# Third attention layer: scores from exact high and low parts, and one list that orders all work between attention blocks

## Chip, cores and metric

The kernel runs on one core of one Trainium2 chip. The metric is device time in microseconds (us) of one execution, here the median of three runs. A profile is of one execution of its own, and its times count from the start of that execution's span.

The engines by the names of the profile: PE is TensorE's matmul, PEld its weight load, DVE is VectorE, ACT is ScalarE, POOL is GpSimd, and SP is the engine that issues most DMAs. SPq and POOLq are the queues of DMA issues.

## What is computed

The reference is a stack of three attention layers and an MLP, on 16 sequences of 256 tokens with 256 features, with 16 heads of 16 features. Cut to what matters:

```
layer 0:  q from rmsnorm(x), k and v from rmsnorm(ctx)
          x = rmsnorm(x + attention(q, k, v) @ Wo)
layer 1:  h = layernorm(x); q, k, v from h, with bias; rope on q and k
          x = x + attention(q, k, v, causal) @ sa_wo + sa_bo
layer 2:  h = layernorm(x); q from h, k and v from ctx, with bias; rope on q and k
          x = x + attention(q, k, v) @ ca_wo + ca_bo
MLP:      x + gelu(layernorm(x) @ fc1 + b1) @ fc2 + b2
```

All inputs and outputs are 32-bit floats. "Third layer" below means layer 2.

## The kernel before

**Tiles.** A sequence b has three attentions, one for each layer, so there are N_ATT = 48 attentions. The digits of ORDER give the layer of each in turn; attention i works on the next sequence of its layer. Sequences at different layers are interleaved, so that one attention's chain of small steps runs beside another one's matmuls. After the 48 attentions eight MLP groups of two sequences follow, from about 700 us on.

**One attention.** `q` and `k` project with `by_feature` (L354), `v` and `project` with `by_token` (L366): 32 records of TensorE each. In layers 1 and 2 `rotated` applies the rope: two biased copies from PSUM on ACT (L475), then on DVE a shuffle (L479) and two products with tables (L483); the sum follows at L514 for q and L591 for k.

The scores of an attention are worked out in blocks: four in layers 0 and 2, three in the causal layer 1. A block ends in two tiles S of two PSUM banks each, and the pool has just two of these. Then two exponentials on ACT (L659) write tiles pt; in layer 1 two `affine_select` on POOL (L666) cut the upper triangle. `values` (L687) multiplies pt with v into tile A; a copy takes it to SBUF (L702).

What follows is a chain through DMAs: `heads_in` (L708) sorts the heads into oT, `sums_in` (L719) takes the softmax sums, `invert` inverts them on DVE (L735) and spreads them through DRAM (L737, L743), and `divide` multiplies (L749). `project` adds the result to x (L755 in layer 0, L758 in the others). For layers 1 and 2 the next attention of the sequence begins with statistics (L266, L267, root on POOL L248 and L249), `norm` (L273) and a transposition, either on TensorE (L288, L298) or as 32x32 pieces on DVE and DMAs (L308, L313, L319). `keep` adds the output bias on POOL (L342).

**Two forms of the scores.** Features of a pair of heads are interleaved over the partitions: even partitions belong to one head, odd ones to the other, 32 partitions to a pair. In the plain form (L637, layers 1 and 2, and the first two attentions) q is copied twice, each copy with the other head's rows set to zero (L515, L518; L522 puts the second copy on ACT), and a true 32-bit matmul of 64 keys and 512 columns gives both heads.

In the fast form (L648; layer 0 from attention 2 on, which `FAST = (0,)` and `fast(i)` choose) k is split exactly into a high part, rounded to the one-pass format float32r, and the rest (`k_high` L553 on ACT, `k_low` L557 on DVE), q likewise (`q_high` L528 on ACT, `q_low` L535 and L538 on DVE). DMAs put the two parts of q (`q_out` L544) and of k (`k_out` L565) in the rows that the masks zeroed. A one-pass matmul of 128 keys and 256 columns then sums, in its 32 rows, both parts of one head's k with one part of its q; two of them (h = 0 and 1) give all four products of that head (i):

```python
for i in range(2):
    at = m * (2 * u + i)
    for h in range(2):
        for r, ps in rows:
            nc.tensor.matmul(
                ps[:, at : at + m],
                lhsT=self.kd[r, i, t, kc * P : (kc + 1) * P].bitcast(F32R),
                rhs=self.qd[r, i, h, t, q0:S].bitcast(F32R),
                start=(h == 0), stop=(h == 1), skip_group_check=True,
            )
```

**What sets the order.** The body stands in `tc.manual_schedule()`: each engine runs its instructions in the order in which the program names them, and semaphores add the waits between engines. The order of the attention stage comes from the loop over i and n (block n of attention i): after `scores(n)` come `values(n - 1)`, and then whole steps of neighbours, by conditions such as `finishing`, `late`, `fresh`, `shifted`, `hasty`. `turned_ahead` chooses which attentions are transposed in pieces. `load_next` issues loads on POOL (L1136) when their turn comes. A step such as `q` is issued as a whole, with its PE, ACT and DVE instructions one after the other.

If a count of softmax sums at the end were too small, a general branch (`shifted_layers`) would run. None of its instructions is in the trace.

Of the kernel before, what the change touches and what calls it, by code (L numbers as in the profile page):

```python
# [30 lines left out]
FAST = (0,)  # L31
# [22 lines left out]

def turned_ahead():


    slots = {}

    def place(j, tried):  # L60
        for m in range(j - 3, max(attended(j)[1] + 2, j - 8), -1):
            if ORDER[m] != 1 and m not in tried:
                tried.add(m)
                if m not in slots or place(slots[m], tried):
                    slots[m] = j
                    return True
        return False

    for j in range(N_ATT):
        if ORDER[j] > 0:  # L70
            place(j, set())
    return slots
# [3 lines left out]
def xattn_kernel(  # L76
# [120 lines left out]
    def fold_bias(items):  # L197

        ps = dense_ps()
        for k in range(KC):  # L200
            for j, (t, at, vcol) in enumerate(items):
                nc.tensor.matmul(
                    ps[32 * j : 32 * j + 32, :D],
                    lhsT=vec[:, vcol + k : vcol + k + 1].to_broadcast([P, 32]),
                    rhs=t[:, k, at : at + D],
                    start=(k == 0), stop=(k == KC - 1), skip_group_check=True,
                )
        sb = work.tile([P, 2 * D], F32, tag="a", name="fold")
        nc.scalar.copy(sb[:, :D], ps[:, :D])
        hop = dram.tile([4, D], F32, tag="fold", name="fold_hop")  # L210
        nc.sync.dma_start(out=hop, in_=sb[0:P:32, :D])
        return hop
# [49 lines left out]
    def ln_stats(src):  # L262
        st = small.tile([P, NC, 6], F32, tag="bst", name="bst")
        mv = small.tile([P, NC, 2], F32, tag="bmv", name="bmv")
        for c in range(NC):
            nc.vector.bn_stats(st[:, c, :], src[:, c, :])  # L266
            nc.vector.bn_aggr(mv[:, c, :], st[:, c, :])  # L267
        return mv, inv_sqrt(mv[:, :, 1], EPS_LN, "ln")
# [25 lines left out]
    def turned(src):  # L294

        ps = turn_ps(src)
        t = turn_tile()
        nc.scalar.copy(  # L298
# [3 lines left out]
        return t  # L302

    def pieces_out(xn):

        t = work.tile([P, 4, KC, NC, 32], F32, tag="a", name="turn")
        for k in range(KC):
# [3 lines left out]
            )  # L311
        hop = dram.tile([P, 4, KC * NC * 32], F32, tag="turn", name="turn_hop")
# [65 lines left out]
    class Att:  # L378
        def __init__(self, i):
            self.i = i  # L380
            self.layer = ORDER[i]
            self.b, self.below = attended(i)
            self.causal = self.layer == 1
            self.w = (w0_sb, sa_sb, ca_sb)[self.layer]
# [12 lines left out]
            self.fast = fast(i)  # L397

        def stats_x(self):
            self.pad = pads[self.b % 2]  # L400
            self.rx = self.pad[0][:, :NC]
            inv_sqrt(mean_squares(self.x, "x"), EPS_RMS, "x", self.rx)

        def stats_y(self):
            self.ry = inv_sqrt(mean_squares(ys.pop(self.b), "y"), EPS_RMS, "y")
# [3 lines left out]
        def stats(self):  # L409
            if self.layer == 0:  # L410
                self.stats_x()
                self.stats_y()
            else:
                self.mv, self.r = ln_stats(self.x)

        def spread(self):
# [3 lines left out]
            for c in range(NC):  # L420
                for j in range(0, P, 32):
# [4 lines left out]
                    )  # L426
            nc.scalar.copy(self.rq, ps[:, :S])

        def send(self):

            if self.layer == 0 and self.i > 1:
                nc.vector.transpose(self.pad[1], self.pad[0])
                self.rq_hop = dram.tile([S], F32, tag="rq", name="rq_hop")
                for c in range(NC):
                    nc.sync.dma_start(
                        out=self.rq_hop[c * P : (c + 1) * P].rearrange("(g j) -> g j", j=32),
                        in_=self.pad[1][c:P:32],
                    )

        def receive(self):  # L440
            if self.layer == 0 and self.i > 1:
                self.rq = work.tile([P, S], F32, tag="rq", name="rq", bufs=1)
                nc.sync.dma_start(out=self.rq, in_=self.rq_hop.partition_broadcast(P))

        def norm(self):
            if self.layer > 0:
                self.xn = ln_apply(self.x, self.mv, self.r, work)

        def keep(self):

            if self.layer > 0:
                add_bias(self.x, R_SAO if self.layer == 1 else R_CAO)

        def turn(self):
            if self.layer == 0:
                self.hT = xTs.pop(self.b)
            else:
                self.hT = turned(self.xn)
            self.kvT = self.hT if self.layer == 1 else yTs[self.b]

        def pieces_out(self):
            self.norm()
            self.hop = pieces_out(self.xn)

        def pieces_in(self):
            self.hT = turn_tile()
            pieces_in(self.hT, self.hop)
            self.kvT = self.hT if self.layer == 1 else yTs[self.b]

        def rotated(self, ps, n):  # L470
# [3 lines left out]
            for t in range(KC):  # L474
                nc.scalar.activation(  # L475
                    a[:, t], ps[:, t], AF.Identity, bias=bias[:, t : t + 1]
                )
            u = work.tile([P, KC, S], F32, tag="u", name="u", bufs=1)
# [3 lines left out]
            for t, table in ((a, cos_t), (u, sin_t)):  # L482
                nc.vector.tensor_tensor(  # L483
                    t, t, table.unsqueeze(1).to_broadcast([P, KC, S]), ALU.mult
                )
            return a, u
# [10 lines left out]
        def q(self, both=True):  # L497
            ps = by_feature(self.hT, self.w, 0)
            if self.fast:
                self.qd = self.query_tile()  # L500
                self.qa = work.tile([P, KC, S], F32, tag="a", name="qa")
                rq = self.rq.unsqueeze(1).to_broadcast([P, KC, S])
                nc.vector.tensor_tensor(self.qa, ps, rq, ALU.mult)
                return
            self.masked_tile()
            if self.layer == 0:
                rq = self.rq.unsqueeze(1).to_broadcast([P, KC, S])
                for i in range(2):
# [4 lines left out]
            a, u = self.rotated(ps, 0)  # L513
            nc.vector.tensor_tensor(a, a, u, ALU.add)  # L514
            nc.vector.tensor_scalar(self.qm[:, :, 0, :], a, parity[0], None, ALU.mult)  # L515
            self.rotated_q = a
            if both:
                nc.vector.tensor_scalar(self.qm[:, :, 1, :], a, parity[1], None, ALU.mult)  # L518

        def second_mask(self):  # L520
            if self.layer > 0 and not self.fast:
                nc.scalar.activation(  # L522
                    self.qm[:, :, 1, :], self.rotated_q, AF.Copy, scale=parity[1]
                )

        def q_high(self):

            nc.scalar.copy(  # L528
# [4 lines left out]
        def q_low(self):  # L533
# [3 lines left out]
            )  # L537
            nc.vector.tensor_copy(self.qd[:, 1, 1].bitcast(F32R), self.qd[:, 0, 1])  # L538
# [7 lines left out]
        def k_mm(self):  # L546
            src = yTs[self.b] if self.layer == 0 else self.kvT
            self.ps_k = by_feature(src, self.w, D)

        def k_high(self):  # L550

            self.hl = work.tile([P, 2, KC, S], F32, tag="hl", name="hl", bufs=1)
# [17 lines left out]
        def first_qk(self):  # L570
# [4 lines left out]
            ps = by_feature(self.hT, self.w, 0)  # L575
            self.spread()
            for t in range(KC):
                nc.scalar.copy(self.kT[:, t], by_feature(self.kvT, self.w, D, [t])[:, t])
            self.stats_y()
# [6 lines left out]
        def k(self):  # L586
            ps = by_feature(self.kvT, self.w, D)
            self.kT = self.key_tile()[:, 0]
            if self.layer > 0:
                a, u = self.rotated(ps, 1)  # L590
                nc.vector.tensor_tensor(self.kT, a, u, ALU.add)  # L591
            else:
                nc.scalar.copy(self.kT, ps)

        def v(self):
            ps = by_token(self.kvT, self.w, 2 * D)
            va = self.va
            if self.layer == 0:
# [3 lines left out]
                )  # L602
                for c in range(NC):
# [5 lines left out]
            else:  # L609
                row = R_SAV if self.layer == 1 else R_CAV  # L610
                nc.gpsimd.memset(va[:, :, :, 1], 1.0)
                nc.vector.tensor_tensor(
# [6 lines left out]
        def scores(self, n):  # L619
# [35 lines left out]
            for ps in pss:  # L655
                pt = work.tile([P, 2, 512], F32, tag="pt", name="pt", bufs=PT_LIVE)
# [3 lines left out]
            for u, unit in enumerate(units):  # L660
                cols = slice(2 * m * u, 2 * m * (u + 1))
                self.pts[unit] = [pt[:, :, cols] for pt in pts]
                if self.causal:
                    for pt in self.pts[unit]:
                        diag = pt.rearrange("p j (i s) -> p j i s", i=2)[:, :, :, 0:P]
                        nc.gpsimd.affine_select(  # L666
                            out=diag, in_=diag, compare_op=ALU.is_ge, fill=0.0, base=0,
                            pattern=[[0, 2], [0, 2], [1, P]], channel_multiplier=-1,
                        )

        def values(self, n):


            for unit in self.parts[n]:
                self.value(*unit)

        def value(self, t, kc):
# [15 lines left out]
            if final and t == 0:  # L693
# [3 lines left out]
                self.take(t, nc.scalar.copy)  # L697
# [6 lines left out]
        def heads_in(self):  # L704

            for t in range(KC):
                for i in range(2):
# [16 lines left out]
        def end(self, copy=nc.vector.tensor_copy):  # L724

            self.take_last(copy)
            self.sums_in()
            self.heads_in()

        def invert(self, beside=lambda: None):  # L730
# [4 lines left out]
            nc.vector.reciprocal(sums[:, 1], sums[:, 0])  # L735
# [1097 lines left out]
```

## Time and profile before

| what | value |
|---|---|
| median of 3 runs (lowest to highest) | 907.46 us (907.29 to 907.56) |
| the profiled execution, its own time | 907.57 us |
| its span | 905.9 us |
| mean granted clock of TensorE | 0.999 |
| TensorE busy, 0 to 20 us | 16.94 us |
| TensorE busy, 40 to 120 us | 76.97 us |
| TensorE busy, 200 to 220 us | 17.93 us |
| DVE busy, all | 689.5 us |
| ACT busy, all | 541.4 us |
| exponentials, layers 1 and 2 (224) | 217.1 us, 1022 ns each |
| exponentials, layer 0 (128) | 135.7 us, 1114 ns each |
| DMA share, mean of 40 to 120 us | 0.51 |

A group's row in the profile reads: line, engine, operation, output <- inputs, shapes, count | busy us, mean ns of one | idle time of the engine just before, and what ended it. A timeline row reads: start us, duration us, engine, line, operation, shapes, count, and in brackets the idle time before it. Consecutive matmuls overlap, so that one group's duration is longer than the step to the next group's start.

### The profile page before, as it was taken

To read this page: it belongs to the slowest core of one execution; us is meant where nothing else is said; L and a number is where in the kernel's file an instruction comes from. 1 tells how busy PE (TensorE), PEld (TensorE's weight loads), DVE (VectorE), ACT (ScalarE), POOL (GpSimd) and SP (SyncE) were. 2 spreads that over 40 slices of the span, in tenths; PEclk is the share of its full clock that TensorE was granted. 3 is DMA by queue.
4 is the path that set the end of the run, shared out by engine and by line. 5 is a ranking of instruction groups with operands and counts; after the bars stand their busy time and mean duration, and the time that the engine had idled before them with its cause. 6 is when DMAs were issued, how large, how long until landed. Compare 5 with 4: busy or idle time off the path is not lost.

```text
span 905.9 us, 32810 instructions
## 1 busy us (share of the span) xinstructions
PE 889.2 (98%) x13762; PEld 538.4 (59%) x13762; DVE 689.5 (76%) x1529; ACT 541.4 (60%) x758; POOL 339.4 (37%) x558
## 2 busy tenths in 40 slices
PE   8999999999999999999999999999999999999997
PEld 3455555445454545455455554444445799999997
DVE  4369878986778887878967889898796687777653
ACT  3776765766676766766666676666665633334440
POOL 4144765425452465244454435556133131111000
PEclk9999999999999999999999999999999999999999
DMA  8454554434243233332354322111211011112201
GB/s 268 151 180 155 169 164 154 132 107 134 79 122 103 97 114 127 95 114 63 109 165 144 119 81 67 63 55 59 62 40 38 26 65 62 54 35 68 71 25 50
DMA packets 94286, 90.26 MB, mean 100 GB/s; under 512 B 25578, under 2 KB 80754, under 8 KB 94130
## 3 DMA queue, kind: packets, MB, share of 16 engines
q1 hardware_dynamic: 89042, 73.11, 25.1%
q0 software_dynamic: 4400, 14.42, 5.4%
q8 instruction: 110, 1.80, 0.8%
q10 hardware_dynamic: 688, 0.54, 0.2%
q14 instruction: 46, 0.38, 0.1%
HBM read 46.33 MB, written 13.65 MB: 66 GB/s over the span
## 4 chain that ended last, share of the span: by engine, by line
PE 84%; DVE 7%; DMA 4%; SPq 2%; issue 1%; ACT 1%; POOL 0%; ACTq 0%; DVEq 0%
PE A L687 16%; PE d L354 16%; PE d L366 14%; PE S L637 13%; PE upX L908 6%; PE A L1006 6%; PE downZ L1006 3%; PE upZ L908 3%; PE S L648 3%; PE d L1006 2%; PE d L908 2%; DMA sums<-av 1%; DVE a L483 1%; DVE u L483 1%; DVE u L479 1%
## 5 line engine op out<-in xcount | busy, mean ns | idle before, releaser
L659 ACT ACTIVATE pt<-S 128x1024 f32<-128x1024 f32 x224 | 217.1, 1022 | 114.8 <-PE S L637 114.8
L687 PE MATMUL A<-pt,va 128*32 128x256 f32 (+1 forms) x3072 | 189.7, 367 | 0.0
L687 PEld LDWEIGHTS A<-pt,va 128*32 128x32 f32 x3072 | 80.6, 109 | 125.1 <-issue 55.2
L659 ACT ACTIVATE pt<-S,sy 128x1024 f32<-128x1024 f32 x128 | 135.7, 1114 | 26.9 <-PE S L648 18.0
L637 PE MATMUL S<-qm,kT 32*64 32x512 f32 (+1 forms) x2176 | 134.5, 559 | 4.0 <-DVE kT L591 3.3
L666 POOL TENSOR_SCALAR_AFFINE_SELECT pt<-pt 128x512 f32<-128x512 f32 x128 | 87.3, 697 | 123.8 <-ACT pt L659 122.8
L475 ACT ACTIVATE a<-d,qk_bias 128x256 f32<-128x256 f32 x128 | 53.7, 470 | 45.4 <-PE d L354 32.9
L342 POOL TENSOR_TENSOR cur<-cur,bias 128x512 f32<-128x512 f32 x48 | 67.4, 1410 | 32.9 <-DVE xn L273 32.8
L248 POOL TENSOR_SCALAR r_ln<-bmv 128x2 f32<-128x2 f32 x48 | 13.5, 281 | 158.0 <-DVE bmv L267 156.8
L637 PEld LDWEIGHTS S<-qm,kT 32*64 32x64 f32 x2176 | 34.4, 130 | 53.1 <-issue 31.9
L354 PE MATMUL d<-hT,sa 128*32 128x256 f32 x1024 | 61.1, 379 | 0.0
L930 ACT COPY g<-upX 128x512 f32<-128x512 f32 x28 | 15.0, 589 | 72.4 <-issue 67.5
L483 DVE TENSOR_TENSOR a<-a,turn 128x512 f32<-128x512 f32 x64 | 52.5, 820 | 2.2
L483 DVE TENSOR_TENSOR u<-u,turn 128x512 f32<-128x512 f32 x64 | 53.9, 842 | 0.0
L702 DVE COPY av<-A 128x512 f32<-128x512 f32 x47 | 31.8, 677 | 22.5 <-PE A L687 22.2
L479 DVE STREAM_SHUFFLE u<-a 128x512 f32<-128x512 f32 x64 | 47.8, 746 | 0.0
L946 ACT ACTIVATE g<-g,fb 128x256 f32<-128x256 f32 x96 | 41.0, 499 | 11.1 <-DVE g L935 11.1
L354 PEld LDWEIGHTS d<-hT,sa 128*32 128x32 f32 x1024 | 33.3, 110 | 22.0
L648 PEld LDWEIGHTS S<-qm,kT 32*128 32x128 f32 x896 | 30.9, 183 | 25.8 <-ACT pt L659 18.6
L648 PE MATMUL S<-qm,kT 32*128 32x256 f32 x896 | 43.2, 303 | 2.3 <-ACT pt L659 1.7
L749 DVE TENSOR_TENSOR oT<-oT,inv 128x512 f32<-128x512 f32 x48 | 36.6, 762 | 7.4 <-DMA oT<-av 5.2
L273 DVE TENSOR_SCALAR xn<-cur,bmv,r_ln 128x256 f32<-128x256 f32 x96 | 40.9, 475 | 0.3 <-POOL r_ln L249 0.3
(167 smaller groups left out, 1655.7 us busy)
## 6 DMA issues: line engine op xcount, KB each, us to landing
inv<-inv_hop SPq DMA_DIRECT2D x96, 128.0 KB
oT<-av SPq DMA_DIRECT2D x192, 64.0 KB
turn_hop<-turn SPq DMA_DIRECT2D x33, 256.0 KB
hT<-turn_hop SPq DMA_DIRECT2D x132, 64.0 KB
kT<-hl SPq DMA_DIRECT2D x28, 256.0 KB
qm<-qm SPq DMA_DIRECT2D x28, 256.0 KB
out<-res SPq DMA_DIRECT2D x15, 256.0 KB
yT<-in_yt POOLq DMA_DIRECT2D x11, 256.0 KB, 3.5
```

The source lines that it names most:

```text
L342: nc.gpsimd.tensor_tensor(t, t, bias_sb[:, row : row + D].unsqueeze(1).to_broadcast([P, NC, D]), ALU.add)
L354: nc.tensor.matmul(o, lhsT=w[:, k, at + t * P + j : at + t * P + j + 32], rhs=tokens, start=(k == 0), stop=(k == KC - 1), skip_group_check ...
L366: nc.tensor.matmul(ps[j : j + 32, c * D : (c + 1) * D], lhsT=some_tokens(src, k, c, j), rhs=w[:, k, at : at + D], start=(k == 0), stop=(k ...
L479: nc.vector.stream_shuffle(u.rearrange("p t s -> p (t s)"), a.rearrange("p t s -> p (t s)"), SWAP)
L483: nc.vector.tensor_tensor(t, t, table.unsqueeze(1).to_broadcast([P, KC, S]), ALU.mult)
L637: nc.tensor.matmul(ps[64 * half : 64 * half + 64, 2 * m * u : 2 * m * (u + 1)] .rearrange("p (i s) -> p i s", i=2), lhsT=self.kT[r, t, at] ...
L648: nc.tensor.matmul(ps[:, at : at + m], lhsT=self.kd[r, i, t, kc * P : (kc + 1) * P].bitcast(F32R), rhs=self.qd[r, i, h, t, q0:S].bitcast(F ...
L659: nc.scalar.activation(pt[:, :, :w], ps[:, :, :w], AF.Exp, scale=scale)
L666: nc.gpsimd.affine_select(out=diag, in_=diag, compare_op=ALU.is_ge, fill=0.0, base=0, pattern=[[0, 2], [0, 2], [1, P]], channel_multiplier=-1,
L687: nc.tensor.matmul(self.av[32 * r : 32 * r + 32, i, q0:S], lhsT=self.va[:, kc, 8 * t + 2 * r + i, :], rhs=pts[r // 2][:, r % 2, i * m : (i ...
L908: nc.tensor.matmul(o if len(b.shape) == 2 else by_groups(o), lhsT=a[:, c * P : (c + 1) * P], rhs=b, start=(first and c % 2 == 0), stop=Tru ...
L1006: nc.tensor.matmul(ps[:, c, :], lhsT=a[f // 2][:, f % 2, c * P : (c + 1) * P], rhs=b[:, f, :], start=(first and c == 0 and f == 0), stop=True,
```

## The change

`FAST` becomes `(0, 2)`, so the third layer takes the fast form too. Its rotated q and k are split as layer 0's are: `q` ends with the sum in tile a, which `q_high` and `q_low` read; `k` writes its sum in the second half of tile hl, `k_high` copies it rounded to the first half, and `k_low` subtracts in place. The two masks of q go in this layer. In layer 1 the second mask is always made on ACT. The tile hl, which had a second use as a buffer for combined MLP weights, loses that one; a part of w0 takes its place, and the general branch loads w0 again.

The methods become generators that yield wherever the engine changes. A string PLAN names all segments, 2,640 words, and each occurrence of a word runs the next segment of that step: `k.11` is named six times, for PE, ACT and four times DVE. The loop with its conditions goes. Transposition in pieces is chosen by the words `pieces` and `turn`, loads by `load_piece`, `load_early` and `load_later`. Start-up (to the first word) and the MLP stage keep their order.

```diff
-FAST = (0,)
+FAST = (0, 2)
...
+PLAN = """
...
+scores.43.0 heads_in.42 q.44 stats.46 values.42.2 scores.43.0 q.44 stats.46 scores.43.0 turn.45
+take_last.42 q.44 turn.45 heads_in.42 scores.43.1 q.44 k_high.44 values.43.0 scores.43.1
+sums_in.42 k_low.44 k.45 q.44 scores.43.1 norm.46 k_out.44 q_high.44 divide.41 scores.43.2 keep.46
+pieces.46 values.43.1 scores.43.2 q_low.44 pieces.46 v.44 v.44 scores.43.2 q_low.44 invert.42 k.45
+q_out.44 divide.42 scores.43.3 v.44 values.43.1 q.45 invert.42 k.45 scores.43.3 k.45 pieces_in.46
+scores.43.3 k.45 values.43.2 q.45 k.45 values.43.3 k_high.45 q.45
...
+        def q(self):
+            ps = by_feature(self.source(False), self.w, 0)
+            yield
...
+            a = self.biased(ps, 0)
+            yield
+            u = self.swapped(a)
+            yield
+            self.times(a, cos_t)
+            yield
+            self.times(u, sin_t)
+            yield
             nc.vector.tensor_tensor(a, a, u, ALU.add)
+            if self.fast:
+                self.qa = a
+                return
+            yield
+            self.masked_tile()
             nc.vector.tensor_scalar(self.qm[:, :, 0, :], a, parity[0], None, ALU.mult)
+            yield
+            nc.scalar.activation(self.qm[:, :, 1, :], a, AF.Copy, scale=parity[1])
...
+        def k(self):
...
+            if self.fast:
+                self.hl = self.high_low()
+                self.ps_k = self.hl[:, 1]
+                nc.vector.tensor_tensor(self.ps_k, a, u, ALU.add)
+                return
...
             pts = []
             for ps in pss:
+                yield
                 pt = work.tile([P, 2, 512], F32, tag="pt", name="pt", bufs=PT_LIVE)
...
-                + [work.tile([P, 2, KC, S], F32, tag="hl", name="down_t", bufs=1)[:, 0]]
+                + [w0_sb[:, 0, : 2 * D].rearrange("p (k s) -> p k s", s=S)]
...
+    def step(word):
+        if word not in steps:
+            steps[word] = begin(word) or iter(())
+        next(steps[word], None)
...
-        for i in range(N_ATT):
-            a, last = att(i), att(i - 1)
...
+        for word in PLAN.split():
+            step(word)
```

## The prediction

> **What bounds the kernel now.** I read the page first: the busy line, then the chain that ended last.
>
> ```profile
> span 905.9 us, 32810 instructions
> ...
> PE 889.2 (98%) x13762; PEld 538.4 (59%) x13762; DVE 689.5 (76%) x1529; ACT 541.4 (60%) x758; POOL 339.4 (37%) x558
> ...
> PE 84%; DVE 7%; DMA 4%; SPq 2%; issue 1%; ACT 1%; POOL 0%; ACTq 0%; DVEq 0%
> ```
>
> TensorE is busy all but 16.7 us, of which 3.1 lie in the first 20 us, and 84% of the chain is its own work. So time is worth what TensorE gets rid of, less any new wait of TensorE. The profiled execution took 907.57 us, 0.1 above the median of 907.46; its span is 905.9, so 1.7 lie around it. I count from 907.57.
>
> Next the groups of instructions, with shapes kept apart, for the two forms of the scores.
>
> ```profile
> L637 PE MATMUL S<-qm,kT 32*64 32x512 f32 x1664 | 116.6, 612 | 4.0 <-DVE kT L591 3.3 <-ACT hT L298 0.7
> L648 PE MATMUL S<-qm,kT 32*128 32x256 f32 x896 | 43.2, 303 | 2.3 <-ACT pt L659 1.7 <-DMA qm<-qm 0.5
> ```
>
> A block outside the causal layer has 16 records in either form, so 1664 records hold 104 block-sized lots (two slow first-layer attentions, the third layer, half of the causal layer) and 896 hold 56 blocks. A mean of one record hides overlap; the step is read from starts in the timeline. First a fast block of layer 0, then a block of layer 2.
>
> ```profile
> 306.66 0.75 PE L648 MATMUL S<-qm,kT 32*128 32x256 f32 x16
> ...
> 307.33 1.07 PE L687 MATMUL A<-pt,va 128*32 128x256 f32 x16
> ...
> 308.22 1.91 PE L366 MATMUL d<-sa,hT 128*32 128x256 f32 x32
> ...
> 310.06 0.75 PE L648 MATMUL S<-qm,kT 32*128 32x256 f32 x16
> ```
>
> ```profile
> 657.70 1.11 PE L637 MATMUL S<-qm,kT 32*64 32x512 f32 x16
> ...
> 658.75 1.07 PE L687 MATMUL A<-pt,va 128*32 128x256 f32 x16
> ...
> 659.64 1.91 PE L354 MATMUL d<-yT,ca 128*32 128x256 f32 x32
> ...
> 661.48 1.11 PE L637 MATMUL S<-qm,kT 32*64 32x512 f32 x16
> ```
>
> Start to start, scores, values and one projection take 0.67 + 0.89 + 1.84 = 3.40 us in the fast form and 1.05 + 0.89 + 1.84 = 3.78 in the other; the usual step of the second kind is 3.77. Nothing else in the block differs, so the form is worth 0.37 us.
>
> **The change, part by part.**
>
> *Scores.* 16 third-layer attentions x 4 blocks x 0.37 = 23.7 us less on TensorE. The instructions are those of L648 in number and shape, so this price is measured and not derived.
>
> The Trainium skill ("FP8 and Floating Point Precision", TensorE Precision Notes) says that a true FP32 product makes four passes. Two one-pass products would then halve the scores, 1.05 to an estimated 0.52, and the 64 blocks would give about 34 us and an end near 874; the rows say 0.67, and I go by them.
>
> *New work on ScalarE.* Each third-layer attention gains q_high (L528, 1.05) and k_high (L553, 0.59): 26.1 us. All 16 second masks of the causal layer now go to ScalarE (L522, 0.72: 11.6), and five masks there go (3.6). ACT ends at 541 + 34 = 575 us. In one block of 3.40 the two exponentials take 1.94 (2 x 0.97 in the timeline), which leaves 1.46, or 5.84 per attention. The rest is two bias pairs (0.84 each), one copy of av (0.60), q_high and k_high: 3.92. It fits, and so I cost it at nothing; but q_high with a second such piece does not fit in one gap.
>
> *New work on VectorE.* q_low (L535 0.69, L538 0.44) and k_low (L557, 0.68) add 1.81 per attention, 28.9 in all. The first mask (L515, 16 of 0.61) and all 27 second masks on VectorE (L518, 0.56) go: 24.9. Net +4. What hides it is TensorE's longer work, but not everywhere:
>
> ```profile
> 540.00:640.00 100.00, 98.34 (x1760) 47.09 (x1760) 91.25 (x165) 64.84 (x88) 55.00 (x69) 1.00 0.20 62
> ```
>
> Columns after the stretch and its length are TensorE, weight loads, VectorE, ScalarE, GpSimd. This stretch has 16 third-layer blocks: TensorE's 100 shrinks by 5.9 to 94.1, while VectorE goes to some 92 (four attentions, each +0.64 or a little more, less up to three masks of the causal layer). So VectorE is 98% of the new stretch. In the last run of third-layer attentions, 653.9 to 684.7 (two attentions), it is 27.5 of 30.8 before, and would be 27.5 + 1.7 = 29.2 against 30.8 - 3.0 = 27.8: 1.4 too much. For eight such attentions that bounds the loss at 5.6, if nothing is moved, and at 0, if the list moves rotations and statistics a block or two. I take 2.
>
> *New transfers.* 64 more issues on SP's queue (q_out L544, k_out L565, 0.58 to 0.62 each): 38 us on a queue that stands waiting for over 400 us in the table of waits. Where q_out waits for q_low, what stands behind it are the head copies, sums and inverses of the attention before, which divide and then project need. In the list divide comes 6.9 us of TensorE work before its project in the median, so nothing is charged. What can be late is q_out itself. The one transfer that TensorE waited for is this:
>
> ```profile
> 351.03 1.16 SPq L544 DMA_DIRECT2D qm<-qm  x2
> ...
> 355.83 0.51 PE L648 MATMUL S<-qm,kT 32*128 32x256 f32 x8 [0.49 <-DMA qm<-qm]
> ```
>
> The second half came 4.8 us after the issue began. In nine others scores started 3.8 to 4.0 after q_out and did not wait. I added up TensorE's steps between q_out.i and scores.i.0 in the list: 27 of 30 attentions have 3.8 or more (rounded), 14 have over 4.8, the shortest (attention 47) has 2.9. If all transfers took 3.8, the loss is under 2 us; if all took 4.8, it is 12.4. I take 0, since none of the other 13 transfers made TensorE wait. The one buffer of hl must be read by k_out before the next k is written to it: the same sum gives 4.3 us at least, and 2.4 is what a kT transfer takes in the chain, so nothing there.
>
> *The order.* The list names the same segments with the same durations; the only new PE instructions are the scores. Its first word is at 16.3 us, so start-up is untouched, and the MLP keeps its order. Every engine runs its words in the listed order, loads on the POOL queue and all of SP's included, so each moved step can gain or lose. TensorE's 13.6 idle us after start-up are what a better order can gain (3.0 of it between 40 and 120, 2.1 between 200 and 220, where hT came late). I summed row durations by attention over the list: VectorE never has over 3.5 us more than TensorE in a run of up to 16 blocks, ScalarE never over 2.1. That excludes an engine overrunning, not a late step. I take 2 of the 13.6 as won, which cancels VectorE's 2.
>
> *Cover by GpSimd.* An operation on VectorE with both inputs in SBUF can be stretched when GpSimd adds the bias:
>
> ```profile
> 666.33 0.69 DVE L483 TENSOR_TENSOR a<-a,turn 128x512 f32<-128x512 f32 x1
> 666.35 1.82 POOL L342 TENSOR_TENSOR cur<-cur,bias 128x512 f32<-128x512 f32 x1
> ...
> 666.94 1.78 DVE L483 TENSOR_TENSOR u<-u,turn 128x512 f32<-128x512 f32 x1
> ```
>
> 0.69 became 1.78: 1.1 us per meeting. The Trainium skill ("SBUF — State Buffer", SBUF: two separate sides) makes it an exclusive lock between a VectorE instruction with two SBUF inputs and a GpSimd one that reads SBUF. That speaks against this change: q_low and now k_low subtract SBUF from SBUF, and if each of the 32 met an add it would cost VectorE about 35 us by the measured 1.1. The 14 q_low of before took 0.68 to 0.69 each and met none.
>
> **Sum.** 907.57 - 23.7 + 2 - 2 = 883.9; I say 884.0.
>
> **Rivals.**
>
> *The list also clears the old waits.* For it: 13.6 us idle, at places with no lack of other work. Against: with 0.37 less per block every wait has less cover. Half of it gives 883.9 - 6.8 = 877. Chance 0.20.
>
> *Late query halves.* Place: the first scores of each fast attention. For: 16 margins below 4.8. Against: the 13 transfers that held nothing up. All at 4.8: 883.9 + 12.4 = 896. Chance 0.20.
>
> *Slower: ScalarE held up by q_high.* It waits for VectorE's rotation, and behind it in ScalarE's queue stand the exponentials; one block takes both score tiles, so the next scores wait too. ScalarE has 1.46 - 1.05 = 0.41 to spare in that block. VectorE late by two bias meetings (2.2) costs 1.8 in each of 16 attentions: 883.9 + 28.6 = 912.5. It decides from 23.7/16 = 1.5 of lost time per attention, a lateness of 1.9. For: VectorE at 98%, and the two buffers of a, where 7 of 99 reuses in the list come within 1.9 us of the last reader. Against: the list puts the third layer's q some 13 to 16 us of TensorE work ahead of its scores, and a path of about 10 us (0.84 + 3.3 + 1.05 + 1.1 + 3.8) leaves room. Chance 0.12.
>
> *No effect.* The list gives back just what the form saves, or the blocks keep 3.77 because scores wait for exponentials (0.87 to their start, 1.94 for them, about 0.4 to the next scores: 3.2, under 3.40). Time 907. Chance 0.03.
>
> **Numbers.** Forecast 884.0 with 0.45. The range 873 to 902: down to most of the idle recovered (0.8 x 13.6 = 10.9), up to the late halves and VectorE's whole 5.6 together (883.9 + 12.4 + 5.6); it leaves out the slower case, no effect and a little of the tails. A measurement here tells about 0.2%, 1.8 us, from no change. Faster 0.45 + 0.20 + 0.20 = 0.85; same 0.03; slower 0.12.
>
> **What would show it.** L648 should have 1920 records and L637 1152; third-layer blocks should step 3.40. A TensorE idle time near 17 us confirms the cancelling, near 10 the first rival. Late halves show as waits of the first L648 of an attention for qm; a held ScalarE as gaps of TensorE before L648 with ACT as releaser and L528 waiting for L514's line. VectorE should be over 95% busy in the stretch that ends the third layer; if TensorE is idle there by more than 5 us, my 2 us were too few. Fast blocks that step over 3.6 would break the main term.

## The result and the profile after

The changed kernel takes 905.9 us (median of 20 runs, 901.97 to 907.44); the kernel before took 909.5 beside it (20 runs, 906.73 to 912.26). The ratio is 0.9958, 95% interval 0.9947 to 0.9969: 3.8 us faster, where 23.5 were forecast. The time lies outside the range of 873 to 902. The profiled execution took 906.3 us, 1.3 less than that of before; the accounting below is of these two executions.

The page of the changed kernel, the lines that answer to those of before:

```profile
span 904.5 us, 32853 instructions
...
PE 881.5 (97%) x13762; PEld 565.6 (63%) x13762; DVE 699.5 (77%) x1534; ACT 570.8 (63%) x801; POOL 352.3 (39%) x558
...
PE 76%; DVE 9%; DMA 5%; ACT 3%; issue 3%; SPq 3%; POOL 1%; ACTq 0%; DVEq 0%; POOLq 0%
```

TensorE is busy 7.7 us less, not 23.7, and idle 23.0 instead of 16.7. Its own share of the chain fell from 84% to 76%: more steps now end in a wait for another engine. The groups of the scores, shapes kept apart:

```profile
L962 PE MATMUL S<-qm,kT 32*128 32x256 f32 x1920 | 96.4, 304 | 6.1 <-ACT pt L974 4.7 <-issue 0.5
L951 PE MATMUL S<-qm,kT 32*64 32x512 f32 x640 | 49.0, 612 | 1.4 <-ACT pt L974 1.2
```

The count is as forecast, and one record takes what it took (304 and 612 ns against 303 and 612). But 1920 records at the price of before, 43.2 for 896, would be busy 92.6 us, and 640 of the plain form 44.8; they are 96.4 and 49.0. Busy time grows with the same records and the same mean when fewer of them overlap. The timeline shows why. TensorE:

```profile
223.60 0.74 PE L962 MATMUL S<-qm,kT 32*128 32x256 f32 x16
224.27 1.93 PE L643 MATMUL d<-cao,oT 128*32 128x256 f32 x32
226.13 1.23 PE L962 MATMUL S<-qm,kT 32*128 32x256 f32 x16
227.29 1.93 PE L1005 MATMUL A<-pt,va 128*32 128x256 f32 x32
```

and ScalarE in the same stretch:

```profile
224.45 2.12 ACT L974 ACTIVATE pt<-S,sy 128x1024 f32<-128x1024 f32 x2 [1.65 <-PE S L962]
226.46 1.05 ACT L821 CAST qm<-a 128x1024 fp32r<-128x1024 f32 x1
227.40 2.13 ACT L974 ACTIVATE pt<-S,sy 128x1024 f32<-128x1024 f32 x2
```

Between the scores at 223.60 and at 226.13 the list puts one projection only. The exponentials start 0.85 after the scores and take 2.12, so the second tile S comes free at 226.57. The next scores begin in the first tile and stand for the second: 1.23 instead of 0.74. It loses 0.49, so the least step between scores that loses nothing is 3.0 us here (2.53 + 0.49). With the third layer's shorter exponentials (1.94) the same step loses 0.22 to 0.31, so it is 2.8 there. The loop of before nearly always puts values and a projection between scores (3.40). Of the steps from scores to scores, 2 of 174 were under 2.95 in the loop; in the list 23 of 173 are.

**Accounting.** I add up the attention stage (from the first scores after 16 us to the MLP's first product) from starts in the timeline: the time of a kind of work runs from its first matmul to the next kind's first, so waits in it and behind it count with it.

| us | before | forecast | after |
|---|---|---|---|
| scores | 166.3 | 142.6 | 159.4 |
| values | 160.5 | 160.5 | 168.9 |
| projections | 344.9 | 344.9 | 341.9 |
| the rest | 12.0 | 12.0 | 11.4 |
| stage | 683.6 | 660 | 681.6 |

The scores gave back 16.8 of 23.7. Call what a block's scores take beyond 0.67 or 1.04 their loss: 5.0 us in all before, 21.8 after (42 blocks of 174 lose over 0.1). I sorted the blocks by what ScalarE did before them: 12.9 of the 21.8 are steps that are too short (8.7 in the 23 steps under 2.95, 2.3 in two blocks at 65 us with nothing between them, the rest in blocks that follow such a step), 5.9 are exponentials that start late behind other work, 2.1 are values that wait, 0.9 small change. This sorting is a reading of the trace. The values' 8.4 are 5.1 of idle time, and a switch: values followed by scores take 0.98, followed by a projection 0.89. The projections gain about what this loses (1.75 ahead of values, 1.84 ahead of scores).

An exponential that starts late looks like this, on ScalarE and then on TensorE:

```profile
412.14 0.64 ACT L873 CAST hl<-hl 128x512 fp32r<-128x512 f32 x1
413.95 0.72 ACT L816 ACTIVATE qm<-a,vec 128x512 f32<-128x512 f32 x1 [1.17 <-DVE a L808]
414.58 2.10 ACT L974 ACTIVATE pt<-S,sy 128x1024 f32<-128x1024 f32 x2
```

```profile
412.23 0.75 PE L962 MATMUL S<-qm,kT 32*128 32x256 f32 x16
412.90 1.93 PE L631 MATMUL d<-hT,ca 128*32 128x256 f32 x32
415.72 2.11 PE L951 MATMUL S<-qm,kT 32*64 32x512 f32 x16 [0.89 <-ACT pt L974]
```

The scores of 412.23 were done by 413. A mask waits 1.17 for VectorE's sum (L808), the exponentials stand behind it, and the next scores lose 0.89 and another 1.0 inside.

### The profile page after: what moved, and what is told of

It reads as the page before. It is cut to its first block, busy times and chain, and to the rows that moved or that the text cites. A ratio compares the mean times of both kernels' runs of the same rounds, so it can differ in the third digit from the quotient of the medians.

```text
span 904.5 us, 32853 instructions
## 1 busy us (share of the span) xinstructions
PE 881.5 (97%) x13762; PEld 565.6 (63%) x13762; DVE 699.5 (77%) x1534; ACT 570.8 (63%) x801; POOL 352.3 (39%) x558
## 4 chain that ended last, share of the span: by engine, by line
PE 76%; DVE 9%; DMA 5%; ACT 3%; issue 3%; SPq 3%; POOL 1%; ACTq 0%; DVEq 0%; POOLq 0%
PE d L643 14%; PE d L631 14%; PE A L1005 13%; PE S L962 7%; PE upX L1219 6%; PE A L1317 6%; PE S L951 5%; PE downZ L1317 3%; PE upZ L1219 3%; ACT pt L974 2%; PE d L1317 2%; PE d L1219 2%; DVE u L772 1%; DMA turn_hop<-bits 1%; SPq L596 1%
## 5 line engine op out<-in xcount | busy, mean ns | idle before, releaser
L1005 PE MATMUL A<-pt,va 128*32 128x256 f32 (+1 forms) x3072 | 186.8, 366 | 5.1 <-DVE av L1020 2.8
L1005 PEld LDWEIGHTS A<-pt,va 128*32 128x32 f32 x3072 | 87.0, 109 | 81.8 <-issue 16.7
L982 POOL TENSOR_SCALAR_AFFINE_SELECT pt<-pt 128x512 f32<-128x512 f32 x128 | 93.4, 750 | 66.5 <-ACT pt L974 65.8
L962 PEld LDWEIGHTS S<-qm,kT 32*128 32x128 f32 x1920 | 68.6, 183 | 56.9 <-issue 29.7
L962 PE MATMUL S<-qm,kT 32*128 32x256 f32 x1920 | 96.4, 304 | 6.1 <-ACT pt L974 4.7
L619 POOL TENSOR_TENSOR cur<-cur,bias 128x512 f32<-128x512 f32 x48 | 65.5, 1368 | 36.5 <-DVE xn L551 36.4
L951 PE MATMUL S<-qm,kT 32*64 32x512 f32 (+1 forms) x1152 | 67.6, 512 | 1.4 <-ACT pt L974 1.2
L1063 POOL TENSOR_TENSOR seen<-seen,sums 128x64 f32<-128x64 f32 x48 | 17.1, 355 | 103.9 <-DVE sums L1049 102.2
L551 DVE TENSOR_SCALAR xn<-cur,bmv,r_ln 128x256 f32<-128x256 f32 x96 | 49.9, 568 | 5.3 <-POOL r_ln L524 5.3
L772 DVE TENSOR_TENSOR a<-a,turn 128x512 f32<-128x512 f32 x64 | 47.5, 742 | 1.8
```

The lines of the kernel that those rows point to most:

```text
L619: nc.gpsimd.tensor_tensor(t, t, bias_sb[:, row : row + D].unsqueeze(1).to_broadcast([P, NC, D]), ALU.add)
L772: nc.vector.tensor_tensor(t, t, table.unsqueeze(1).to_broadcast([P, KC, S]), ALU.mult)
L951: nc.tensor.matmul(ps[64 * half : 64 * half + 64, 2 * m * u : 2 * m * (u + 1)] .rearrange("p (i s) -> p i s", i=2), lhsT=self.kT[r, t, at] ...
L962: nc.tensor.matmul(ps[:, at : at + m], lhsT=self.kd[r, i, t, kc * P : (kc + 1) * P].bitcast(F32R), rhs=self.qd[r, i, h, t, q0:S].bitcast(F ...
L982: nc.gpsimd.affine_select(out=diag, in_=diag, compare_op=ALU.is_ge, fill=0.0, base=0, pattern=[[0, 2], [0, 2], [1, P]], channel_multiplier=-1,
L1005: nc.tensor.matmul(self.av[32 * r : 32 * r + 32, i, q0:S], lhsT=self.va[:, kc, 8 * t + 2 * r + i, :], rhs=pts[r // 2][:, r % 2, i * m : (i ...
```

## The experiments

Each ratio is to the kernel before, measured beside it, with its 95% interval. Theory A: the list costs what the form saves, because its scores wait for exponentials. The rivals: the new splitting work (B), VectorE and GpSimd locking each other out (C), a list with no slack on VectorE (E).

**list_plain and loop_fast: one half of the change each.** The first is the changed kernel with `FAST = (0,)`, the third layer's masks in the places of `q_low` and its `q_high`, `k_high`, `k_low`, `q_out`, `k_out` dropped (its keys, in the plain form, go from hl to kT by one DMA in the place of `k_out`). The second is the loop of before with `FAST = (0, 2)` and the splitting added where layer 0 has it.

```diff
-FAST = (0, 2)
+FAST = (0,)
...
-pieces.13 load_piece.9.1 q_high.11 scores.10.2 stats.12 values.10.1 q_low.11
+pieces.13 load_piece.9.1 scores.10.2 stats.12 values.10.1 q.11
```

> The list with the third layer in the plain form: its two masks stand where q_low's two steps stood (VectorE, ScalarE), k goes from hl to kT by one DMA at k_out's place. Theory A, the list's order is what gives the gain back (TensorE reaches the next scores before ScalarE has read the score tiles): the 64 blocks cost 0.37 more again, and most of the waits stay, so 905.9 + 23.7 less some 5 of waits that longer scores cover: 920 to 927, well above the kernel before. Theory B, the fast form's own work on ScalarE and VectorE makes the waits: without it the list is as good as the loop, 905 to 909. Theory C, GpSimd's adds stretch VectorE: they stand where they stood, so as A.

```diff
-FAST = (0,)
+FAST = (0, 2)
...
+            if self.fast and self.layer == 2:
+                a, u = self.rotated(ps, 0)
+                nc.vector.tensor_tensor(a, a, u, ALU.add)
+                self.qd = self.query_tile()
+                self.qa = a
+                return
```

> The loop of before with the third layer in the fast form (k of attention i+2 projected and split in attention i, as for layer 0). Theory A: the loop keeps values and one projection between scores, so most of the 23.7 comes: 884 to 893. Theory B: the extra work on ScalarE and VectorE makes the same waits in any order: 902 to 908. Theory C: between, 893 to 902, since VectorE meets GpSimd's adds here too.

list_plain: 926.3 us, 1.0191 (1.0172 to 1.0210). The list without the fast form costs 17 us (with it come the second masks of the causal layer, all on ScalarE, and the DMA above), and within the list the form saves 1.0191 - 0.9958, 21 us of the 23.7. Its groups, for the same records as before (116.6 and 43.2 there):

```profile
L929 PE MATMUL S<-qm,kT 32*64 32x512 f32 x1664 | 127.1, 613 | 3.0 <-ACT pt L952 2.7 <-DVE kT L838 0.3
L940 PE MATMUL S<-qm,kT 32*128 32x256 f32 x896 | 45.1, 305 | 3.0 <-ACT pt L952 2.4
```

The loss of the scores is 20.9 with no new splitting work in the kernel, and the values take 168.2, as in the change; so B is not needed for either.

loop_fast: 1005.3 us, 1.1052 (1.1014 to 1.1090). Every part of the theories missed by 100 us. In the loop q is projected one attention ahead, its rotation is issued as a whole, and `q_high` stands in front of exponentials while VectorE is not there yet:

```profile
185.72 1.03 ACT L670 ACTIVATE pt<-S 128x1024 f32<-128x1024 f32 x1
...
188.20 1.65 DVE L501 TENSOR_TENSOR a<-a,u 128x512 f32<-128x512 f32 x1
...
189.93 1.04 ACT L534 CAST qm<-a 128x1024 fp32r<-128x1024 f32 x1 [3.17 <-issue]
190.88 1.93 ACT L670 ACTIVATE pt<-S 128x1024 f32<-128x1024 f32 x2
```

The profile names no releaser for `q_high`, but the sum that it reads (L501) ends at 189.85. Scores waited 67.3 us for exponentials at their start (59 waits). Not all of the 97 us is waits: TensorE is idle 91.0 us where it was 16.7, and it is also busy 912.1 where it was 889.2, at a mean granted clock of 0.962 in place of 0.999. This order does not carry the fast third layer, so the two halves do not add up. The mechanism is that of my slower rival, in the other order.

**loop_late: q_high and k_high one block later in that loop.**

```diff
-                    if fast(i + 1) and a.causal:
+                    if fast(i + 1) and a.causal and att(i + 1).layer == 0:
                         do(i + 1, "q_high")
...
+                if n == 2:
+                    if fast(i + 1) and att(i + 1).layer == 2 and not a.causal:
+                        do(i + 1, "q_high", "q_low", "q_out")
+                    if i > 0 and fast(i + 2) and att(i + 2).layer == 2:
+                        do(i + 2, "k_high", "k_low")
```

(The third layer's `k_out` moves into the next attention.)

> The old loop with the third layer in the fast form, as in loop_fast, but q_high, k_high and what follows them come one block later for the third layer. Theory A (in loop_fast the exponentials stood behind q_high and k_high, which themselves waited 1.5 to 4 us for VectorE's rotation): the waits of fast scores for exponentials fall from 76 us to under 20, and the time from 1005 to 930 or less, to about 890 if nothing else is late. Rival: VectorE itself is too slow for the rotation and the low parts within an attention, and the waits only move to the next attention's first scores: over 960.

1000.9 us, 1.1006 (1.0965 to 1.1048), at the same granted clock of 0.962: the time is the rival's, and the waits moved as it said, from exponentials to the transfer that now starts late:

```profile
PE S L659 <- DMA qm<-qm: 64.8, 18, 6.5
...
PE S L659 <- ACT pt L670: 8.4, 17, 1.1
```

Columns of the waits: total us, number, longest. In the first place q's halves are in ScalarE's way, in the second they are late. That VectorE is too slow for any place, the rival's cause, is not shown: only these two were tried.

**list_fast_nobias: GpSimd's bias adds away.** `keep` does nothing, so the output biases of layers 1 and 2 are left out.

```diff
-            add_bias(self.x, R_SAO if self.layer == 1 else R_CAO)
+            pass
```

> The kernel after without GpSimd's 48 minus 16 bias adds of the attention stage (keep does nothing: the output bias of layers 1 and 2 is left out). Theory C, VectorE is late because those adds stretch it to 1.8 us: the waits in the scores fall from 22.5 us to under 10 and the time to 890 to 896. Theory A: ScalarE's exponentials are where they were, 902 to 906. Theory B: as A, with VectorE a little freer: 900 to 905.

909.2 us, 1.0017 (0.9998 to 1.0036). VectorE's products with the sine table fell from 831 to 764 ns each, those with the cosine table from 742 to 720, so GpSimd's adds did stretch them; but the time did not fall (the mean granted clock was 0.993, where the change had 0.997), and the scores still lose 20.7. C is out.

**list_exp_half and before_exp_half: exponentials over half of the columns.**

```diff
-                nc.scalar.activation(pt[:, :, :w], ps[:, :, :w], AF.Exp, scale=scale)
+                x = w if self.causal else w // 2
+                nc.scalar.activation(pt[:, :, :x], ps[:, :, :x], AF.Exp, scale=scale)
...
-                        rhs=pts[r // 2][:, r % 2, i * m : (i + 1) * m],
+                        rhs=pts[r // 2][:, r % 2, (i * m if self.causal else 0) :][:, :m],
```

> The changed kernel, with the exponential taken over half of the columns in the blocks of layers 1 and 3; the product with the values reads that half twice, so the attention of those layers is not what the reference computes, while every instruction of TensorE stays as it is. Theory A (the 21.8 us that the scores lose are waits for the exponentials of the block before): the loss falls under 7 us and the time by 14 to 20 us, to 886 to 892. Rival (the scores are slowed by something else, as traffic in SBUF or PSUM or the clock): loss over 15, time over 900.

> A control for list_exp_half: the kernel of before with the same half exponentials in layers 1 and 3 (and the same double reading in the product with the values). Theory A (the list's scores wait for exponentials, the loop's hardly do): the loop has 5.0 us of such loss in all, so it gains at most 4 us: 903 to 908. Rival (half exponentials help any order of this kernel alike, by unloading ScalarE or PSUM): it gains the 7 us of the list too, 898 to 901.

(The blocks shortened are those of the first and the third layer, 0 and 2 in the reference's count; the causal layer keeps its whole exponentials.) The list: 899.2 us, 0.9895 (0.9866 to 0.9924), 0.6% below the change. The loop: 908.95, 0.9993 (0.9971 to 1.0015), nothing. ScalarE loses 106 us of work in the list, and the list's fast scores change so:

```profile
L962 PE MATMUL S<-qm,kT 32*128 32x256 f32 x1920 | 91.4, 303 | 3.9 <-DMA qm<-qm 1.4 <-ACT pt L975 1.2 <-ACT av L1021 0.9
```

From 96.4 with 6.1 idle to 91.4 with 3.9, below the 92.6 of before. Exponentials do hold up the list's scores and not the loop's, as A says. The size misses: 6 us by the ratios, not 14 to 20, and a loss that fell from 21.8 to 14.3, nearer to the rival's figures than to A's. What speaks for A is where it fell: behind the blocks with half exponentials from 15.5 to 6.2. Behind causal blocks, whose exponentials were left whole, a thing that I had not taken off, it is 8.1, where it was 6.3.

**list_less_dve and before_less_dve: the sine product away (64 instructions of VectorE).**

```diff
             self.times(a, cos_t)
             yield
-            self.times(u, sin_t)
             yield
```

> The changed kernel without the product of the swapped part with the sine table (64 of VectorE's instructions, 53.2 us), so its rotation isn't the reference's. Theory A (ScalarE's loop of exponentials is what the list's scores wait for, VectorE is not): within 3 us of the changed kernel, 903 to 908. Theory E (VectorE, in step with a list that leaves it no slack, holds ScalarE's words and the takes): the time falls by 5 to 12 us, to 894 to 901.

> A control for list_less_dve: the kernel of before without the product of the swapped part with the sine table (64 of VectorE's instructions, so the rotation isn't the reference's). Theory: the list has no slack left on VectorE while the loop has, so the loop gains at most 4 us (904 to 908) where the list gained 7. Rival: 53 us less of VectorE help any order alike, 898 to 902; then the list's own loss has nothing to do with VectorE.

The list: 898.9 us, 0.9870 (0.9843 to 0.9898), so 0.9% below the change, as E said. But the loop: 901.9, 0.9937 (0.9917 to 0.9957), 0.6%. The two gains are alike within their intervals. In the loop the scores' waits for VectorE's keys go:

```profile
L637 PE MATMUL S<-qm,kT 32*64 32x512 f32 (+1 forms) x2176 | 134.2, 560 | 0.0
```

(4.0 of idle time before.) With 53 us less work for VectorE either order is some 6 to 8 us faster; E does not explain what the list costs over the loop. The list's scores still lose 19.4 without the sine product.

**list_spaced and list_even: more TensorE work between scores.** In list_spaced over 200 words of TensorE are pulled ahead, values among them, so that fewer places have under 2.6 us of work between two scores (20, where the change has 38; the moves also change what some words read). In list_even some 40 projections move by one or two blocks, and nothing else.

> The kernel after with TensorE's words moved within the list, no other engine's: where less than 2.6 us of TensorE work stands between the scores of two blocks (38 of 174 places), the next free projection or values is pulled ahead; 92 intervals then hold values and one projection (68 before) and 20 hold less. Theory A: waits in the scores fall by half or more, 890 to 899. Theory B or C: ScalarE and VectorE run as before, 902 to 908, or slower, since pulled words can wait for inputs.

> The changed kernel with some 40 projections of TensorE moved by one or two blocks, so that fewer blocks have under 2.3 us of other work between their scores; ScalarE's order untouched. By the durations the moves take away about a third of what short intervals cost. Theory A2: the loss falls by 4 to 7 us, time 899 to 902. Theory A1: no change, 904 to 908.

1056.7 us, 1.1651 (1.1613 to 1.1689), and 926.4 us, 1.0183 (1.0145 to 1.0222): both far off. In the first, values wait where scores had waited:

```profile
PE A L987 <- ACT pt L956: 47.7, 82, 1.3
PE A L987 <- ACT av L1002: 38.6, 22, 3.3
```

In the second the loss rose to 30.5, with exponentials started late. I take the cause to be that a projection's place on TensorE sets when its biased copies and rotation can run, and that their places on ScalarE and VectorE had stayed; no run shows it. Neither run tests the short steps alone.

**list_unblocked: ScalarE's words behind the exponentials.**

```diff
-q_high.8 scores.7.1 heads_in.6 scores.7.0 send.10 project.4 scores.7.0 project.5 send.10
-scores.7.1 stats_y.10 q_low.8 heads_in.6 scores.7.1 q_low.8 scores.7.1 v.8 project.5 stats.11
+scores.7.1 heads_in.6 scores.7.0 send.10 project.4 scores.7.0 project.5 send.10
+scores.7.1 stats_y.10 heads_in.6 scores.7.1 q_high.8 q_low.8 q_low.8 scores.7.1 v.8 project.5 stats.11
```

> The changed kernel with 14 of ScalarE's words (q_high, biases, second masks that were seen to run ahead of waiting exponentials by over 0.3 us) moved behind the block's two exponentials, TensorE's order untouched. Theory A1 (most of the loss is ScalarE's queue): the loss falls by about 8 us, time 897 to 900. Theory A2 (most is too little TensorE work between two blocks' scores): it falls by under 3, time 902 to 907.

913.4 us, 1.0071 (1.0050 to 1.0092): slower than the change by 1.1%. Exponentials late by over 0.3 us went from 15 to 8 by my count, as meant, but the loss rose to 24.4, which neither theory expected. What came instead is on VectorE, since words that follow a moved one move with it:

```profile
PE A L987 <- DVE av L1002: 8.4, 7, 2.6
PE S L944 <- ACT pt L956: 4.6, 8, 1.3
```

The first was 2.8 in the change.

**list_qhigh_pool: q_high on GpSimd.**

```diff
-            nc.scalar.copy(
+            nc.gpsimd.tensor_copy(
```

> The changed kernel with all 30 copies of q_high made by GpSimd instead of ScalarE (31 us of ScalarE's), in the same places of the list. Theory A1 (q_high in ScalarE's queue is what delays exponentials, each time it waits for VectorE): the loss falls by 3 to 6 us, to 900 to 903. Rival 1 (ScalarE's queue is not it; short intervals between scores are): 904 to 908. Rival 2 (the copy is slower on GpSimd and q_low, which waits for it, holds VectorE): over 910.

912.95 us, 1.0052 (1.0030 to 1.0074): rival 2 by the time. The copy takes 1.12 us in place of 1.05, q_low beside it 0.94 in place of 0.82, and the loss stays at 21.9. So q_high in ScalarE's queue is not the cause of the loss; what makes this version 0.9% slower than the change was not traced further.

**list_three: three words, three waits.**

```diff
-stats.5 scores.3.3 v.4 v.4
+stats.5 v.4 scores.3.3 v.4
...
-sums_in.9 pieces.13 load_piece.9.1 q_high.11 scores.10.2 stats.12
+sums_in.9 stats.12 pieces.13 load_piece.9.1 q_high.11 scores.10.2
...
-scores.38.1 invert.36 take_last.37
+scores.38.1 invert.36
```

(`take_last.37` now stands 10 words earlier, ahead of the rotation's first product.)

> The changed kernel with three words of its list moved: v.4 ahead of the scores that follow scores.3.2 without other work between (loss 2.3 us at 65), the statistics of turn.12 ahead of pieces.13 on VectorE (TensorE's idle 1.8 us at 168), and take_last.37 ahead of the rotation of q.39 on VectorE (2.1 us at 562). If each wait can be mended where it stands: 1.8, 0.8 and 2.1 less, and 1.5 more if the clock's dip at 172 goes, so 899 to 902. Rival (the list has no slack, a wait taken away in one place comes back in another, as in list_unblocked): 904 to 910.

905.4 us, 0.9945 (0.9926 to 0.9964): 1 us below the change and inside its interval, so faster than before but not shown to be faster than the change. At two of the three places the wait went: the gap of 2.3 after 65, and the values at 562. The transposition's wait fell from 1.74 to 1.03. Then, 8 us after the place of the second, this stands where no wait was:

```profile
567.07 1.91 PE L625 MATMUL d<-sao,oT 128*32 128x256 f32 x32
569.90 2.02 PE L933 MATMUL S<-qm,kT 32*64 32x512 f32 x16 [0.92 <-ACT pt L956]
```

The loss over the stage was 22.4, no less than the 21.8, in a profiled execution that was the longest of the ten (909.7). No version here beats both kernels by more than its interval.

## Why the prediction was wrong

*The sign was right, the size was not.* The sign owes something to luck: it is the difference of 21 us saved and 17 lost, and the 17 were not foreseen. By its steps:

- **The scores' 23.7.** Right within a tenth: 21 in list_plain against the change. Where the list puts values and a projection between scores, the step is what I said, 3.41 (670.33, 673.74, 677.14, 680.55 in the timeline).
- **The order, "I take 2 of the 13.6 as won".** This step failed. The list in place of the loop costs 17 us (list_plain). I had excluded "an engine overrunning, not a late step", priced only the first, and put the second at a gain. TensorE's idle time went to 23.0 where 17 was to confirm it. Sums by attention cannot show it: in mine ScalarE was never over 2.1 us behind, while a single step of 2.5 us is too short for its 2.8 to 3.0.
- **No effect, 0.03.** Its first cause is what happened: the list gives back most of what the form saves. For its second I had the numbers, 0.87 + 1.94 + 0.4 = 3.2, and compared them with the mean step of the loop, 3.40, rather than with the steps in the list. There, 29 pairs of neighbouring scores have 1.84 us or less of other TensorE work between them; 0.67 + 1.84 is 2.51. That count could be had from the list before the run. It deserved the weight that I gave to a list clearing the old waits.
- **ScalarE's new work at nothing.** Nearly right for the work itself: the loss is there without it (20.9 in list_plain), and taking q_high away from ScalarE leaves it at 21.9. What I wrote of the queue behind q_high holds, but gaps behind late words are only 5.9 us of the loss, of which masks and biases have a share. The marks that I had set for the slower rival, gaps with ScalarE as releaser and q_high waiting for the rotation, are there (q_high waits 7.2 us for L808, five times); they are worth a fifth of its 28.6.
- **VectorE, 2 us in the tail.** Wrong, harmlessly: from 653 to 684 us it is busy 27.0 of 31.0, and TensorE has no idle time there. The list has put rotations earlier: 104.2 of 120 between 320 and 440, where it was 96.9. Over the whole it is busy 10.0 us more and not 4, in part because the 96 norms take 568 ns each, where they took 475.
- **Late query halves.** Did not happen: of TensorE's waits for qm there is one, of a weight load, 0.3 us. In loop_late, where the place of q_out did move, they cost 64.8.
- **The lock.** Rightly left out. The 14 q_low of layer 0 take 0.69 again, the 16 new ones 0.82, some 2 us in all.
- **Two sums.** The upper bound adds VectorE's whole 5.6 to a sum that already has 2 of them, and the first rival takes half of the idle time off a sum that already has 2 of it. Neither changes the outcome.

The Trainium skill ("PSUM — Partial Sum Buffer", Engine vs sequencer instructions) says that the queues of ScalarE, VectorE and GpSimd are strictly first in, first out, and that matmuls keep their order too. The rows at 412 to 415 agree: a mask that waits 1.17 holds exponentials whose scores are done. In an order written out by hand each word is therefore a possible wait for all behind it, and the moves above show that.

**What is open.** That the loss is mostly short steps (12.9 of 21.8) is read from the trace, not shown by a run: the half exponentials show that exponentials are waited for in the list and not in the loop, and recover 6 us, and both attempts to lengthen the steps moved other waits as well. Whether another list keeps the loop's 5.0 of loss and carries the fast third layer, which would end near the forecast, was not found.

## What to carry to other kernels

Before pricing a new order, take the shortest loop between two engines that share few buffers (here scores, two exponentials, two tiles), and compare it with every step of the new order, not with the mean. Two kernels that differ in an order and in a form need the order alone as a run of its own. In this list of in-order engines a wait was seldom removed by moving one word: three mended places gave 1 us of 5.

## What was not expected of the hardware

After TensorE's idle time of 1.74 us at 168 the granted clock was 0.50 for 3.4 us, from 171.9 on, and one projection took 3.15 us instead of 1.91:

```profile
168.00:171.00 3.00, 1.26 (x20) 0.64 (x16) 2.21 (x5) 2.88 (x6) 1.54 (x3) 1.00 0.70 258
171.90:175.30 3.40, 3.40 (x36) 1.70 (x32) 3.26 (x9) 2.38 (x3) 1.96 (x3) 0.50 0.56 152
175.40:178.80 3.40, 3.40 (x72) 1.96 (x68) 1.32 (x3) 0.84 (x2) 2.26 (x5) 1.00 0.50 150
```

(The column before the last two is the clock.) The Trainium skill ("TensorE: Matmul & The Clock Gate", Part 1) ties the drop to an idle window of about 3.4 us; this one was half as long. After an idle time of 2.04 at 563 the clock stayed at 1.00, and so it did after the same 1.74 in list_unblocked. So it is not the length alone; what decides was not found. It cost some 1.7 us, 1.2 in this projection and 0.5 in the values before it.
